# Two banded layers on one core: inverse roots from GpSimd to VectorE, some norm columns from ScalarE to GpSimd, no bias pass in layer two, and a written order for each layer

## The chip, the cores and the metric

The kernel runs on one core of a Trainium2 chip. A core has TensorE (PE, with its weight loads, PEld), VectorE (DVE), ScalarE (ACT), GpSimd (POOL) and SyncE (SP, which here only issues DMAs). Each engine executes its own queue in order. The metric is the device time of one execution in microseconds. Before the change three runs took 4815.11, 4811.23 and 4803.99 us; the median is 4811.23 us. One more execution was taken with the profiler and is the source of every other time below.

## The reference

The input x is 512 x 512 positions with 64 channels. Two layers follow each other, and each is `x = x + conv(_gn(x))`: `_gn` normalizes the channels in 32 groups of two over all positions, and `conv` computes, per position:

```python
xn = _ln(x, norm_scale, norm_bias)                              # over 64 channels
left  = (xn @ Wl + bl) * mask * sigmoid(xn @ Wlg + blg)         # 64 -> 128
right = (xn @ Wr + br) * mask * sigmoid(xn @ Wrg + brg)
out_gate = sigmoid(xn @ Wog + bog)
out = _banded_ingoing(left, right, WIN)       # row i: sum over rows i-4..i+4 of right
out = _ln(out, out_norm_scale, out_norm_bias) * out_gate        # over 128 hidden channels
return out @ Wo + bo                                            # 128 -> 64
```

So each position needs two inverse square roots per layer: one for the norm over 64 input channels and one for the norm over 128 hidden channels.

## The kernel before

**Tiles.** A *unit* is a tile `z` of 128 partitions by 8 columns by 64 channels: 64 rows of the image at 8 columns of its left half on partitions 0 to 63, and the same rows at 8 columns of its right half on partitions 64 to 127. Nine blocks of 64 rows, two chunks of 128 columns in each and 16 units in a chunk make 288 units per layer. An *out* is the same 8 columns on their way out, also 288 per layer. A buffer `RO` holds the projected right side of almost two chunks, and after the band step the same place holds its result.

**Steps.** `layer` (L739) runs a loop over steps t. Step t takes unit t through the projections (`right`, `right_gate`, `right_end`), transposes unit t+1 (`transposed`, `kept`), normalizes unit t+2 (`inner_norm`, L436) and, further ahead, applies the group norm to a unit (`affine`, L427: one multiplication by `ga`, one addition of `gb`) and collects its statistics (`inner_stats`). The band product of a chunk (`mix`, L567, 16 matmul groups and two copies of 128x512 back to `RO` for each) is spread over the steps of the next chunk: per 16 steps six have two of these bands, four have one and six have none. An out with number t leaves LAG = 30 steps after its chunk began: `out_stats` (four statistics instructions), `norm` (L631, one step ahead: eight ScalarE instructions of 128x128, one per column), `gates` and `gated` (matmul and sigmoid of the output gate), `turned` (transposes), `times_gate`, `end` (last product) and, a step later, `ended` (adds the product to the residual tile `XR` and issues the store). In layer one `sums` also accumulates the statistics of the next layer's group norm on PE.

**Inverse roots.** Every fourth step `solve` (L598) takes the variances that have been collected, usually 32 columns of inputs and 32 of outs, so tiles of 128x64. Five small VectorE instructions prepare variances, negated means and a first guess by integer arithmetic; then `rsqrt` (L134) runs ten instructions on GpSimd, and two more there multiply by the mask. All lie in SBUF. `inner_norm` and `norm` read the result `rs` (and `nm`) of the group.

**Residual.** `fetch` loads the 8 columns of the layer's input again into one of four tiles `XR`. `biased` (L698) adds a constant row to it on GpSimd, in both layers: `bo`, and a shift that keeps the intermediate image near zero mean.

**PSUM.** Eight banks. In layer one: three single banks that take turns, two pairs of banks that take turns, and one bank that holds the sums. In layer two: four single banks and two pairs. `right` and `transposed` use pairs; `gates`, `turned`, `end` and both halves of each `mix` use single banks.

**Order.** The instructions are issued through `en`, which keeps program order on every engine, so the text of the loop body (L835 to L910) is the order of every queue. Both layers use the same text. SP's queue issues per step the loads of `z`, `XR`, `A` and `zg` ahead of the body, and the stores of `later` (in `kept`) and of the image (in `ended`).

Of the kernel before, what the change touches and what calls it, by code (L numbers as in the profile page):

```python
# [8 lines left out]
F32 = mybir.dt.float32  # L9
# [7 lines left out]
P = 128  # L17
WIN = 4
# [12 lines left out]
LN_EPS = 1e-6  # L31

# [47 lines left out]
def tile_two_banded_layers(  # L80
# [35 lines left out]
    nc.vector.memset(all_ones, 1.0)  # L116
    ones_row = const.tile([1, P], F32, name="ones_row")
# [16 lines left out]
    def rsqrt(o: bass.AP, v: bass.AP, vec=nc.vector, e=nc.vector):  # L134


        p, n = v.shape
        t, u = (
            sm.tile([P, 3 * NB], F32, tag=f"rsqrt{i}", name="rsqrt", bufs=1)[:p, :n]
            for i in range(2)  # L140
        )
        vec.tensor_scalar(
            o.bitcast(I32), v.bitcast(I32), -0.5, float(0x5F3759DF), ALU.mult, ALU.add
        )
        e.tensor_tensor(t, o, o, ALU.mult)
        e.tensor_tensor(t, t, v, ALU.mult)
        e.tensor_scalar(u, t, -10.0 / 3.0, None, ALU.add)
        e.tensor_tensor(t, t, u, ALU.mult)
        e.tensor_scalar(t, t, 5.0, None, ALU.add)
        e.tensor_tensor(o, o, t, ALU.mult)  # L150
        e.tensor_tensor(t, o, o, ALU.mult)
        e.tensor_tensor(t, t, v, ALU.mult)
        e.tensor_scalar(t, t, -27.0 / 1024.0, 0.5625, ALU.mult, ALU.add)
        e.tensor_tensor(o, o, t, ALU.mult)


    PARTS = (
        ("right", 2 * H), ("left", 2 * H), ("gate", H), ("Wo", D), ("ob", 1), ("add", 2 * D),
# [60 lines left out]
    def solve_layer(i: int, f: dict, r: dict, tmp, half: bass.AP):  # L219
# [36 lines left out]
        add = r["add"].rearrange("p (t c) -> p t c", c=D)  # L256
        nc.vector.tensor_copy(add[:, 0, :], pb[:, :D])
# [15 lines left out]
        nc.vector.tensor_tensor(r["m2"], r["m"], r["m"], ALU.mult)  # L273

# [7 lines left out]
    def shifted(i: int, r: dict, tmp):  # L282
        add = r["add"].rearrange("p (t c) -> p t c", c=D)
        if i == 0:

            bias = tmp.tile([P, G], F32, name="bias")
            nc.vector.tensor_reduce(
                bias, add[:, 0, :].rearrange("p (g t) -> p g t", t=2), AX.X, ALU.add
            )
            nc.vector.scalar_tensor_tensor(bias, bias, 0.5, total, ALU.mult, ALU.add)  # L290
            spread(shift, bias)
        op = ALU.add if i else ALU.subtract
        nc.vector.tensor_tensor(add[:, 0, :], add[:, 0, :], shift, op)
        nc.vector.tensor_copy(add[:, 1, :], add[:, 0, :])


# [6 lines left out]
    shift = const.tile([P, D], F32, name="shift")  # L303
# [4 lines left out]
    def group_affine(mean: bass.AP, var: bass.AP, pool):  # L308

        ve = pool.tile([P, D], F32, name="g_ve")  # L310
        nc.vector.tensor_scalar(ve, var, GN_EPS, None, ALU.add)
        rsqrt(ga, ve)
        nc.vector.scalar_tensor_tensor(gb, mean, -1.0, ga, ALU.mult, ALU.mult)
# [113 lines left out]
    def affine(u: Unit, engine):  # L427

        engine.tensor_tensor(u.z, u.z, mid(ga, JU), ALU.mult)
# [6 lines left out]
    def inner_norm(u: Unit):  # L436
        z = u.z.rearrange("p (k t) c -> p k t c", t=2)
        m = u.mean.unsqueeze(3).broadcast_to([P, JU // 2, 2, D])
        en.gpsimd.tensor_tensor(z, z, m, ALU.subtract)
# [127 lines left out]
    def mix(c: int, A: bass.AP, h0: int) -> list:  # L567
# [6 lines left out]
        ph = [one_bank().rearrange("i (h t j) -> i h t j", h=q, t=2) for s in range(2)]  # L574
# [23 lines left out]
    def solve(w: dict, ins: list, outs: list, sti, sto):  # L598

        ni, no = len(ins) * JU, len(outs) * JU  # L600
        v = sm.tile([P, 3 * NB], F32, tag="var", name="var", bufs=1)[:, : ni + no]
        r = sm.tile([P, 3 * NB], F32, tag="rs", name="rs", bufs=3)[:, : ni + no]
        if ni:
            en.vector.tensor_scalar(
                v[:, :ni].rearrange("p (k t) -> p k t", t=2), sti[:, : ni // 2, 2::3],
                1.0 / D, LN_EPS, ALU.mult, ALU.add,
            )
            for n, u in enumerate(ins):
                u.rs = r[:, n * JU : (n + 1) * JU]
        if no:  # L610

            js = slice(outs[0].m, outs[0].m + no)
            vo = v[:, ni:]
            en.vector.scalar_tensor_tensor(
                vo.rearrange("p (k t) -> p k t", t=2), sto[:, :, 2::3], 1.0 / H,
                w["m2"][:, js].rearrange("p (k t) -> p k t", t=2), ALU.mult, ALU.mult,
            )
            en.vector.tensor_scalar(vo, vo, LN_EPS, None, ALU.add)
            nm = sm.tile([P, NB], F32, tag="nm", name="nm")[:, :no]
            en.vector.tensor_scalar(  # L620
                nm.rearrange("p (k t) -> p k t", t=2), sto[:, :, 1::3], -1.0, None, ALU.mult
            )
        rsqrt(r, v, en.vector, en.gpsimd)
        if no:
            ro = r[:, ni:]
            en.gpsimd.tensor_tensor(ro, ro, w["m"][:, js], ALU.mult)
            en.gpsimd.tensor_tensor(nm, nm, ro, ALU.mult)
            for n, o in enumerate(outs):
                o.rs, o.nm = ro[:, n * JU : (n + 1) * JU], nm[:, n * JU : (n + 1) * JU]
# [417 lines left out]
```

## Time and profile before

| | |
|---|---|
| median of 3 runs | 4811.23 us |
| profiled execution | 4808.51 us, span 4806.5 us |
| busy, whole span | PE 3796.6, DVE 3929.9, ACT 3708.4, POOL 3817.1 us |
| DMA | 983.63 MB, mean 205 GB/s |
| full-load part of layer one, 600 to 2300 us | PE 1555, DVE 1459, ACT 1521, POOL 1560 us busy of 1700 |
| full-load part of layer two, 2900 to 4600 us | PE 1432, DVE 1511, ACT 1492, POOL 1576 us busy of 1700 |

All operations of the loop carry one line, L373, since a helper issues them; they are told apart by the names of their tiles. `z<-z,ga` reads: writes z, reads z and ga. `on<-RO,nm,rs` is `norm`, `ZH<-bank,pack,gate` is `times_gate`, `XR<-XR,fewer` and `XR<-XR,pack` are `biased`, `RO<-banks,sg` is `right_end`, `RO<-bank` are the copies of `mix`, `zT` is `kept`, `sto` and `sti` are statistics. In a group's line the number after the bar is the busy time in us, then the mean duration of one instruction in ns, then the idle time of the engine just ahead of these instructions and what ended it. In a line of the timeline the first number is the start in us and the second how long the piece lasts; the idle time ahead of it stands in brackets.

### The profile page before, as it was taken

How to read it: one execution, taken by the hardware profiler on the slowest of the kernel's cores; microseconds unless marked ns; L12 is line 12 of the kernel's file. 1: busy time of each engine (PE TensorE's matmuls, PEld its weight loads, DVE VectorE, ACT ScalarE, POOL GpSimd, SP SyncE). 2: the span in 40 equal slices, each digit the busy share in tenths (PEclk: the TensorE clock that was granted, in tenths of full speed). 3: DMA queues.
4: the chain of work that ended last, by engine and by line, in shares of the span. 5: the costliest groups of instructions: out<-in, count | busy, mean ns of one | idle time of the engine just before them, and what ended most of it. 6: DMA issues, size and time to landing. Idle time of an engine off the chain costs nothing. (4 is left out here: it accounts for less than half of the span.)

```text
span 4806.5 us, 193543 instructions
## 1 busy us (share of the span) xinstructions
PE 3796.6 (79%) x76306; PEld 3293.0 (69%) x76306; DVE 3929.9 (82%) x9635; ACT 3708.4 (77%) x8732; POOL 3817.1 (79%) x4739
## 2 busy tenths in 40 slices
PE   1025799989999999999985478888888888888888
PEld 0024688878888887888854467777777777777775
DVE  6954788888888888888867478888888888888887
ACT  0013689888888898989883268888888888888899
POOL 0035999999999999999734589999999999999964
PEclk9997999999999999999997689999999999999999
DMA  7859677777777777777763967777777777777876
GB/s 299 336 178 108 172 212 213 215 210 215 211 209 210 211 214 212 214 212 215 199 170 100 105 168 212 216 214 209 217 213 215 213 213 218 210 216 211 222 200 179
DMA packets 1437651, 983.63 MB, mean 205 GB/s; under 512 B 167202, under 2 KB 1284424, under 8 KB 1432392
## 3 DMA queue, kind: packets, MB, share of 16 engines
q1 hardware_dynamic: 1432064, 969.75, 73.6%
q8 instruction: 604, 9.90, 0.9%
q14 instruction: 303, 2.48, 0.2%
q10 hardware_dynamic: 4680, 1.50, 0.1%
HBM read 658.42 MB, written 312.46 MB: 202 GB/s over the span
## 5 line engine op out<-in xcount | busy, mean ns | idle before, releaser
L373 ACT ACTIVATE on<-RO,nm,rs 128x128 f32<-128x128 f32 x4608 | 1927.7, 496 | 15.3 <-PE bank L373 9.9
L373 PEld LDWEIGHTS banks<-pack,zT 64*128 64x128 f32 x18576 | 1251.3, 195 | 549.5 <-ACT zT L373 288.9
L373 PE MATMUL banks<-pack,zT 64*128 64x128 f32 x18576 | 1365.6, 289 | 272.8 <-ACT zT L373 222.6
L373 DVE TENSOR_TENSOR RO<-banks,sg 128x512 f32<-128x512 f32 (+1 forms) x1188 | 795.3, 673 | 228.3 <-POOL sg L373 116.2
L373 DVE SCALAR_TENSOR_TENSOR ZH<-bank,pack,gate 128x448 f32<-128x448 f32 (+1 forms) x1152 | 741.6, 685 | 173.3 <-PE bank L373 97.3
L373 ACT ACTIVATE sg<-banks 128x512 f32<-128x512 f32 (+1 forms) x1188 | 698.0, 589 | 188.6 <-PE banks L373 188.2
L373 DVE BATCH_NORM_STATS2 sto<-RO 128x6 f32<-128x256 f32 x2304 | 800.8, 411 | 3.7
L373 POOL TENSOR_TENSOR z<-z,gb 128x512 f32<-128x512 f32 x536 | 684.8, 1278 | 42.0
L373 PE MATMUL bank<-RO,A 64*64 64x128 f32 x18432 | 706.0, 292 | 3.9 <-ACT RO L373 2.4
L373 PE MATMUL bank<-pack,ZH 128*64 128x64 f32 x18432 | 694.6, 231 | 5.0 <-ACT gate L373 4.1
L373 POOL TENSOR_TENSOR z<-z,ga 128x512 f32<-128x512 f32 x536 | 685.6, 1279 | 3.2 <-DMA z<-mid_x 1.9
L373 POOL TENSOR_TENSOR z<-z,rs 128x512 f32<-128x512 f32 x586 | 619.3, 1057 | 46.0
L373 DVE COPY RO<-bank 128x512 f32<-128x512 f32 x576 | 398.4, 692 | 310.6 <-PE bank L373 307.3
L373 PEld LDWEIGHTS bank<-pack,ZH 128*64 128x64 f32 x18432 | 612.6, 143 | 47.3 <-ACT gate L373 8.5
L373 POOL TENSOR_TENSOR z<-z,sti 128x512 f32<-128x512 f32 x586 | 627.9, 1072 | 0.0
L373 PEld LDWEIGHTS bank<-RO,A 64*64 64x64 f32 x18432 | 582.0, 142 | 43.0 <-ACT RO L373 4.1
L373 ACT ACTIVATE gate<-bank 128x448 f32<-128x448 f32 (+1 forms) x1152 | 565.8, 545 | 34.5 <-PE bank L373 32.0
L373 ACT ACTIVATE zT<-banks 128x512 f32<-128x512 f32 (+1 forms) x1084 | 463.5, 481 | 139.6 <-PE banks L373 128.9
L373 PE MATMUL bank<-zg,pack 64*128 64x448 f32 (+1 forms) x2304 | 564.3, 556 | 4.6 <-DMA zg<-later 4.6
L373 ACT COPY RO<-bank 128x512 f32<-128x512 f32 x576 | 333.2, 579 | 282.3 <-PE bank L373 282.1
L373 PE MATMUL banks<-ident,z 64*128 64x64 f32 x4336 | 254.1, 233 | 359.2 <-DVE RO L373 336.9
L373 DVE BATCH_NORM_STATS2 sti<-z 128x6 f32<-128x128 f32 x2344 | 500.5, 280 | 15.2 <-POOL z L373 14.2
(144 smaller groups left out, 3908.6 us busy)
## 6 DMA issues: line engine op xcount, KB each, us to landing
later<-zT SPq DMA_DIRECT2D x576, 256.0 KB
A<-left_of SPq DMA_DIRECT2D x1152, 128.0 KB
zg<-later SPq DMA_DIRECT2D x576, 256.0 KB
z<-in_x_dram SPq DMA_DIRECT2D x576, 128.0 KB
z<-mid_x SPq DMA_DIRECT2D x576, 128.0 KB
gn_x<-in_x_dram SPq DMA_DIRECT2D x16, 4096.0 KB
XR<-in_x_dram SPq DMA_DIRECT2D x448, 112.0 KB
mid_x<-XR SPq DMA_DIRECT2D x448, 112.0 KB
```

What stands on the lines that cost most here:

```text
L373: return lambda *a, **k: tc.keep_in_program_order(f(*a, **k))
```

## The change

Six things change together.

1. `solve` returns two parts. `prepare` issues on ScalarE one activation that writes the inputs' variances to `var` in SBUF, and two that write the outs' variances and negated means to a PSUM bank. `roots` issues on VectorE 14 instructions in place of five on VectorE and twelve on GpSimd. Its operands alternate between a PSUM bank and SBUF, with at most one SBUF tensor as input of each.
2. `norm` gives the last column (layer one) or the last two columns (layer two) of each out to GpSimd, as one `tensor_scalar` of 128x128 per column.
3. `biased` is no longer called in layer two: `both`, the sum of the two layers' `bo`, is added in layer one, and `mid_stats` takes the second layer's `bo` out of the statistics with six small VectorE instructions. The shift is gone.
4. In layer one both halves of a band lie in one pair of banks; in layer two they stay in two single banks.
5. In layer one the second copy of a second band goes to ScalarE.
6. The loop body is read from a list, one per layer. `affine` and `inner_norm` are split in two calls each, so that the list can place them apart. `prepare` ("solve on a") and `roots` ("solve on d") stand near the end of the step.

```diff
+FIRST = [
+    ("out stats", 2), "gates", "gated", ("project", 0), ("project", 4), "turn",
+    ("sigmoid", 0), ("out stats", 3), "scale", ("right", 0), ("sigmoid", 4),
+    ("norm", (0, 4)), "norm columns", "centre", "move", "last product", ("right", 4),
+    "times gate", "rescale", "transpose", ("out stats", 99), "inner stats", "keep", "solve",
+    "end", ("band", 0), ("copy a", 0), "sums", "bias", ("band", 1), ("copy b", 0),
+    ("solve on", "a"), "scale next", "move next", ("norm", (4, 8)), ("copy a", 1),
+    ("solve on", "d"), ("copy b", 1),
+]
+SECOND = [
+    ("out stats", 3), "scale", ("out stats", 2), "gates", ("project", 0), "gated",
+    ("sigmoid", 0), ("project", 4), ("out stats", 99), ("right", 0), ("sigmoid", 4), "turn",
+    ("norm", (0, 4)), "last product", "norm columns", "centre", "scale next", "rescale",
+    "times gate", "transpose", ("band", 0), "keep", "move next", "end", ("right", 4),
+    ("copy b", 0), "inner stats", "solve", "move", ("copy a", 0), ("band", 1),
+    ("solve on", "a"), ("copy b", 1), ("copy a", 1), ("norm", (4, 8)), ("solve on", "d"),
+]
...
-        ph = [one_bank().rearrange("i (h t j) -> i h t j", h=q, t=2) for s in range(2)]
+        if APART[0 if stats else 1]:
+            pb = [one_bank() for s in range(2)]
+        else:
+            two = two_banks()
+            pb = [two[:, s * 512 : (s + 1) * 512] for s in range(2)]
...
+        def prepare():
+            held.extend((one_bank(), temporary("var")))
+            bank, v = held
+            if ni:
+                en.scalar.activation(
+                    pairs(v[:, :ni]), sti[:, : ni // 2, 2::3], AF.Identity, bias=ln_eps,
+                    scale=UP / D,
+                )
+            if no:
+                en.scalar.copy(pairs(bank[:, 6 * NB : 6 * NB + no]), sto[:, :, 2::3])
+                en.scalar.mul(pairs(bank[:, 7 * NB : 7 * NB + no]), sto[:, :, 1::3], -1.0)
+
+        def roots():
+            bank, v = held
+            y, s = bank[:, :n], bank[:, 3 * NB :][:, :n]
+            t, u = temporary("rsqrt_t"), temporary("rsqrt_u")
+            vec = en.vector
+            if no:
+                vo, mean = (bank[:, k * NB : k * NB + no] for k in (6, 7))
+                vec.tensor_tensor(vo, vo, w["m2"][:, js], mult)
+                vec.tensor_scalar(v[:, ni:], vo, LN_EPS * UP, None, add)
+            vec.tensor_scalar(
+                y.bitcast(I32), v.bitcast(I32), -0.5, float(0x5F3759DF - 2**31), mult, add
+            )
+            vec.tensor_tensor(u, y, v, mult)
+            vec.tensor_tensor(t, y, u, mult)
+            vec.tensor_tensor(s, y, u, mult)
+            vec.scalar_tensor_tensor(u, t, -10.0 / 3.0, s, add, mult)
+            vec.scalar_tensor_tensor(y, u, 5.0, y, add, mult)
+            vec.tensor_tensor(u, y, v, mult)
+            vec.tensor_tensor(t, y, u, mult)
+            c = -0.5625 * 1024.0 / 27.0
+            if ni:
+                vec.scalar_tensor_tensor(r[:, :ni], t[:, :ni], c, y[:, :ni], add, mult)
+            if no:
+                vec.scalar_tensor_tensor(y[:, ni:], t[:, ni:], c, y[:, ni:], add, mult)
+                vec.tensor_tensor(ro, y[:, ni:], w["m"][:, js], mult)
+                vec.tensor_tensor(nm, mean, ro, mult)
...
+            if pool:
+                en.gpsimd.tensor_scalar(to, of, rs, nm, ALU.mult, ALU.add)
+            else:
+                en.scalar.activation(to, of, AF.Identity, bias=nm, scale=rs)
...
+                elif name == "norm" and t + 1 in outs:
+                    lo, hi = n
+                    norm(outs[t + 1], lo, min(hi, JU - nv), False)
+                elif name == "norm columns" and t + 1 in outs:
+                    norm(outs[t + 1], JU - nv, JU, True)
```

Here `nv` is 1 in layer one and 2 in layer two, and `APART` is false in layer one and true in layer two.

## The prediction

> **What bounds the kernel now.** I read the page's busy table first (four engines within 82% and 77%: no verdict), then the stretches of full load, then GpSimd's groups in them, the waits and the timeline.
>
> ```profile
> 600.00:2300.00 1700.00, 1555.34 (x32978) 1372.73 (x32977) 1459.31 (x3598) 1521.02 (x3542) 1560.42 (x1885) 0.98 0.76 212
> 2900.00:4600.00 1700.00, 1432.20 (x29446) 1255.82 (x29439) 1510.81 (x3630) 1492.26 (x3568) 1576.47 (x1907) 0.96 0.77 214
> ```
>
> After the window come its length, then PE, PEld, DVE, ACT, POOL, the granted clock, the DMA share and GB/s. GpSimd is highest in both layers (92 and 93%). Its groups between 800 and 2300 us:
>
> ```profile
> L373 POOL TENSOR_TENSOR z<-z,ga 128x512 f32<-128x512 f32 x208 | 265.9, 1278 | 0.0
> L373 POOL TENSOR_TENSOR z<-z,gb 128x512 f32<-128x512 f32 x207 | 264.6, 1278 | 16.2
> L373 POOL TENSOR_TENSOR XR<-XR,fewer 120x512 f32<-120x512 f32 x188 | 223.5, 1189 | 0.3 <-DMA XR<-in_x_dram 0.2
> L373 POOL TENSOR_TENSOR z<-z,sti 128x512 f32<-128x512 f32 x208 | 219.7, 1056 | 0.0
> L373 POOL TENSOR_TENSOR z<-z,rs 128x512 f32<-128x512 f32 x208 | 216.9, 1043 | 16.3
> L373 POOL TENSOR_SCALAR rsqrt<-rsqrt 128x64 f32<-128x64 f32 x156 | 50.9, 326 | 13.6
> L373 POOL TENSOR_TENSOR rsqrt<-rs 128x64 f32<-128x64 f32 x104 | 30.4, 292 | 47.1 <-DVE rs L373 43.0
> ```
>
> Its only real wait is 43.0 us, for VectorE's first guess; the other idle time is gaps of about 0.08 us. The five large operations and their gaps are 1247 us, 5.99 per step over 208 steps. The root groups (seven, of which two stand above) are 190 us busy and 90 idle: 280 / 52 solves = 5.4 us, 1.35 per step. Together they fill the window. GpSimd is the bound, and the others wait for what it delays:
>
> ```profile
> 1508.51 0.18 DVE L373 SCALAR_TENSOR_TENSOR var<-sto,pack 128x32 f32<-128x32 f32 x1
> 1508.72 1.20 DVE L373 TENSOR_SCALAR var<-var 128x32 f32<-128x32 f32 x1
> 1510.23 0.29 POOL L373 TENSOR_TENSOR rsqrt<-rs 128x64 f32<-128x64 f32 x1 [0.35 <-DVE rs L373]
> 1510.87 0.35 PEld L373 LDWEIGHTS banks<-ident,z 64*128 64x128 f32 x8 [2.83 <-POOL rsqrt L373]
> 1514.54 0.25 POOL L373 TENSOR_TENSOR nm<-nm,rs 128x32 f32<-128x32 f32 x1
> ```
>
> A solve also makes VectorE wait: a 128x32 operation that takes 0.18 us elsewhere took 1.20 beside a GpSimd operation, and PE stood still 2.8 us. Period of 16 steps, from the last product of the same step: layer one 116.2 us (1442.59 to 1558.83), layer two 114.3 (half of 3507.19 to 3735.74):
>
> ```profile
> 1442.59 1.15 PE L373 MATMUL bank<-pack,ZH 128*64 128x64 f32 x32
> 1558.83 1.15 PE L373 MATMUL bank<-pack,ZH 128*64 128x64 f32 x32
> 3735.74 1.15 PE L373 MATMUL bank<-pack,ZH 128*64 128x64 f32 x32
> ```
>
> What the other engines need of a period is its length times the share in which they don't wait in the table of waits. Layer one (1500 us): PE waits 127, so 106.4; ACT 161: 103.7; DVE 208: 100.1. Layer two: PE 236: 96.3; ACT 186: 100.1; DVE 160: 102.1.
>
> **The change, per 16 steps (four solves).**
>
> *Roots.* GpSimd loses 4 x 5.4. VectorE loses five instructions (77.6 us / 52 = 1.49 per solve in layer one; 114.6 / 53 = 2.16 in layer two, where contention weighs more) and gains 14 dependent ones. The nearest row is the root chain that runs on VectorE between the layers, same width, twelve instructions in 2.87 us from the first's start to the next operation's:
>
> ```profile
> 2563.90 0.20 DVE L142 TENSOR_SCALAR ga<-on 128x64 int32<-128x64 int32 x1
> 2564.12 0.22 DVE L145 TENSOR_TENSOR rsqrt<-ga 128x64 f32<-128x64 f32 x1
> 2566.77 0.68 DVE L373 TENSOR_TENSOR z<-z,ga 128x512 f32<-128x512 f32 x1
> 2560.60 0.21 DVE L931 TENSOR_TENSOR on<-acc,ident 64x64 f32<-64x64 f32 x1
> ```
>
> 0.239 each, 3.35 per solve; the last line has a PSUM operand and takes no longer. Bounds: 0.11 each (spacing of independent ones, 2 us less) to 0.50 (mean of the `var` rows beside GpSimd, 7.0 per solve). I take 3.35. Net +7.4 (layer one), +4.8 (layer two). The chain stands at the step's end; behind it queue the next step's statistics and first `right_end`, which frees the banks that PE needs.
>
> [...]
>
> *Prepare.* Three small activations. Nearest row 128x128 at 0.42 busy; I take 0.3 (0.2 to 0.42): ACT +3.6. It waits for the last statistics, with two norm columns and band copies behind it.
>
> *Norm columns.* ACT loses 0.42 per column (697.0 / 1661): -6.7, -13.4. GpSimd pays between 0.33 (128x64 scalar row) and 1.04 (a 128x512 row, 18 times on `sg`); by width and a gap I take 0.5: +8, +16. New wait: the columns need the previous out's transposes done, so GpSimd can no longer run ahead of PE's step; centring and rescaling queue behind, but their reader is the transpose one step later, some 4 us of cover. Without the cover, that wait returns to PE.
>
> [...] Here the giver is ACT, so 0.5 against 0.42 buys balance. [...]
>
> *Bias.* GpSimd loses 1.19 x 16 in layer two: its four operations on `z` remain, 268.9 + 268.4 + 220.5 + 218.0 us and 33 of gaps in 2900 to 4400 us, 4.80 per step over 210. In that layer's tail its wait for the `XR` loads (40 us after 4620) goes too; next in line is `ended`, which reads the same tile a step later, so I count nothing there. The six operations in `mid_stats` stand in the open between the layers: 6 x 0.239 = 1.4 us, less the few that set up the shift.
>
> *Band copies.* Layer one: six of 16 copies move, DVE -3.7 (spacing 0.61), ACT +3.5. Pairs instead of single banks: the pair users per step become projections 2, transpose 1, band 1; hidden behind the six PE groups of a step while copies keep pace; a late copy holds the next projection, and at the worst one copy (0.6 us) per two-band step shows, 6 x 0.6 = 3.6 per period.
>
> *Orders, bank rings.* No work, only waits; bounded below nothing by the better packing and above by the slower case among the rivals. On SP the stores stay behind the same instructions (`later` behind `keep`, the image behind `end`) and the loads ahead of the body; the number of issues per step does not change. The DMA share of 0.76 and 0.77 rises with the pace to about 0.81; a wait of PE, ACT, DVE or POOL for a load is at most 0.2 us now in full load, so I take nothing; the bound above is a late `z` load holding GpSimd, which the tails show for `XR` (up to 12.5 us once).
>
> Needs after, layer one: PE 106.4, POOL (5.99 + 0.5) x 16 = 103.8, DVE 100.1 + 7.4 - 3.7 = 103.8, ACT 103.7 - 6.7 + 3.5 + 3.6 = 104.1. Layer two: DVE 106.9, PE 96.3, POOL (4.80 + 1.0) x 16 = 92.8, ACT 90.3. The bound engine now gets 97% of the time (43 us lost of 1500); with that, 106.4 / 0.97 = 109.7 and 106.9 / 0.97 = 110.2. Gain 6.5 and 4.1 per period. Units and outs run together in steps 30 to 287, 16.1 periods per layer: 105 + 66 = 171 us. Ends: the last 16 steps of layer two go at 4.02 us, ACT-bound on eight columns (16 x 0.6 = 10); the steps before and layer one's tail 10; the two starts (GpSimd 90% busy) 5 each. Sum 171 + 30 - 1 = 200. The profiled execution's 4808.5 less 200 is 4608; the median lies 3 us above it: **4610 us**.
>
> **Rivals.**
>
> - *Better packing* (0.15): PE's 106.4 holds stretched weight loads. From the timeline, undisturbed steps take 7.95 (two bands) and 6.27 (one); with 5.45 for none, 6 x 7.95 + 4 x 6.27 + 6 x 5.45 = 105.5. At 106 in both layers: 16.1 x 18.5 + 30 = 328, so 4480.
> - *Waits take the place* (0.16): four near-equal engines get 94%: 113.2, 113.7; 16.1 x 3.6 + 30 = 88: 4725. A norm column at 0.75 in layer one gives (5.99 + 0.83) x 16 / 0.97 = 112.5, much the same.
> - *Slower: the root chain is not covered* (0.14). Place: the end of each fourth step, 0.9 of prepare plus 3.35, with PE waiting for the banks behind it, as it waited 2.8 us at 1510. Layer one's 105.5 + 4 x 4.25 = 122.5 against 116.2; layer two's undisturbed 102 (7.16, 6.25, 5.69 per step) + 17 = 119. 16.1 x 11 - 30 = +147: 4960. It decides from 2.7 us (layer one) and 3.1 (layer two) exposed per solve. Against it: roots are needed only by the next step's norms and rescaling, after its sigmoids, 3.5 us in.
> - *No difference* (0.02).
>
> Forecast's own case, 4540 to 4680: 0.53. A measurement tells 0.2%, some 10 us. Faster 0.15 + 0.16 + 0.53 = 0.84. Below 4480 I leave 0.07; the slower case starts at 4822 and reaches to 4960, and I keep the range to 4820, leaving 0.13.
>
> **What would show it.** GpSimd's `rsqrt` groups gone, VectorE with about 14 instructions of 0.2 per solve and no `var` row near 1 us; GpSimd's busy share in layer two near 84%, VectorE's near 95% and highest; PE's waits for POOL (75 and 61 us per 1500) gone; 16 steps near 110 us in both layers; 128x128 columns on POOL near 0.45. Wrong if PE's waits for VectorE grow beyond the present 97 and 167 us per 1500, if columns cost 1 us, or if the chain's instructions take 0.4 or more.

## The result and the profile after

The changed kernel takes 4767.63 us (median of 4 runs, 4746.72 to 4776.52), the kernel before 4813.17 us beside it (4803.99 to 4817.25): a ratio of 0.9897, 95% interval 0.9879 to 0.9915. It is 1% faster, where 4% was forecast. The profiled execution takes 4769.15 us, span 4767.2.

The two stretches of full load after, with the same columns as before (window, length, PE, PEld, DVE, ACT, POOL, clock, DMA share, GB/s):

```profile
600.00:2300.00 1700.00, 1581.22 (x32602) 1373.64 (x32602) 1466.38 (x3985) 1507.07 (x3528) 1421.86 (x1398) 0.98 0.76 210
2900.00:4600.00 1700.00, 1495.45 (x29730) 1302.58 (x29726) 1542.81 (x4175) 1424.44 (x3296) 1281.06 (x1429) 0.96 0.78 215
```

GpSimd is no longer the fullest engine: 1422 and 1281 us in place of 1560 and 1576. PE is now, in layer one (1581 us), and VectorE in layer two (1543), but the time hardly fell. Some of the groups between 800 and 2300 us:

```profile
L381 POOL TENSOR_SCALAR on<-RO,rs,nm 128x128 f32<-128x128 f32 x207 | 93.4, 451 | 232.0 <-PE bank L381 113.9 <-ACT sg L381 110.4 <-DVE nm L381 6.3
L381 DVE TENSOR_TENSOR rsqrt_u<-bank,var 128x64 f32<-128x64 f32 x102 | 22.9, 224 | 3.5
L381 DVE SCALAR_TENSOR_TENSOR bank<-rsqrt_t,bank 128x32 f32<-128x32 f32 x51 | 10.0, 196 | 1.8
L381 PE MATMUL bank<-zg,pack 64*128 64x448 f32 (+1 forms) x824 | 253.0, 605 | 62.8 <-DMA zg<-later 55.0 <-DVE sto L381 3.2 <-DVE sti L381 2.8
```

The norm column costs 0.451 us, the root chain's instructions 0.19 to 0.23 us, and GpSimd waits 232 us, which is its slack. The last line is new: the matmuls of `gates` (`bank<-zg,pack`) wait for the load of `zg`, the gate's input that `recall` reads back from memory. The table of waits (engine, what it waited to do, for whom; total, times, longest) between 2900 and 4400 us has more of it. In the kernel before there was none, neither there nor between 800 and 2300 us:

```profile
PE bank L381 <- DMA zg<-later: 96.8, 48, 4.4
PEld bank L381 <- DMA zg<-later: 50.0, 22, 4.5
```

One such wait in the timeline (start, duration):

```profile
1544.31 0.55 SPq L381 DMA_DIRECT2D zg<-later  x1
1548.12 1.87 PE L381 MATMUL bank<-zg,pack 64*128 64x448 f32 x4 [3.02 <-DMA zg<-later]
1549.75 2.62 PE L381 MATMUL banks<-pack,zT 64*128 64x128 f32 x32
1550.04 0.98 ACT L381 ACTIVATE gate<-bank 128x448 f32<-128x448 f32 x2 [3.31 <-issue]
1552.20 0.69 DVE L381 TENSOR_TENSOR RO<-banks,sg 128x512 f32<-128x512 f32 x1 [4.00 <-ACT sg L381]
1553.06 0.45 POOL L381 TENSOR_SCALAR on<-RO,rs,nm 128x128 f32<-128x128 f32 x1 [4.91 <-ACT sg L381]
```

SP issued the load at 1544.31, and PE took its data 3.8 us later, after 3.0 us of standing still. ACT, VectorE and GpSimd then wait in turn. In the new lists `gates` is among PE's first work of a step; before it stood behind the first `right` products.

Pair the n-th `zg` load of a trace with the n-th out's gate product, and take the time from the start of the issue to the start of the product. In the two stretches of full load its median was 9.7 and 8.6 us before and is 6.3 and 5.3 us now. Where PE waited for the load now, this time was at least 2.99 us, so no load that PE waited for was there sooner. Before, one product in 475 started less than 4 us behind the issue; now 90 of 472 do. This one was the shortest before, with 3.85 us and no wait:

```profile
3613.06 0.56 SPq L373 DMA_DIRECT2D zg<-later  x1
3616.91 0.92 PE L373 MATMUL bank<-zg,pack 64*128 64x448 f32 x4
```

The stall has a second price, in the granted clock (column behind the busy times):

```profile
1548.10:1551.50 3.40, 3.38 (x24) 2.64 (x26) 0.10 (x1) 0.98 (x2) 0.05 (x1) 0.56 0.91 255
```

For 3.4 us behind the stall the clock is 0.56, and the projections take 2.62 us, where they took 1.95 to 2.18 us in the three steps before. A shorter pause has the same behind it: 1.92 us ahead of 3209.41, with a clock of 0.50 from 3209.99 to 3213.40, and projections of 3.39 us.

Where did the 39 us of the profiled executions go? Measured from the first to the 257th last product of a layer, 16 steps went from 115.4 to 116.3 us in layer one and from 114.0 to 113.9 in layer two: 11 us more over 16 such periods in each layer. The ends gained 50 us: the first last product comes 27 us earlier (519.9 in place of 547.0), the stretch from layer one's last to layer two's first of them is 18 us shorter (261.5 in place of 280.0), the two tails 2.6 and 1.9. So the steady state, in which 171 us were forecast, gained nothing.

### The profile page after: what moved, and what is told of

It reads as the page before. It is cut to its first block, busy times and chain, and to the rows that moved or that the text cites. A ratio compares the mean times of both kernels' runs of the same rounds, so it can differ in the third digit from the quotient of the medians.

```text
span 4767.2 us, 193179 instructions
## 1 busy us (share of the span) xinstructions
PE 3885.2 (81%) x76306; PEld 3337.2 (70%) x76306; DVE 4007.1 (84%) x10943; ACT 3608.6 (76%) x8410; POOL 3274.7 (69%) x3427
## 3 DMA queue, kind: packets, MB, share of 16 engines
q1 hardware_dynamic: 1432064, 969.69, 74.4%
## 5 line engine op out<-in xcount | busy, mean ns | idle before, releaser
L381 ACT ACTIVATE on<-RO,nm,rs 128x128 f32<-128x128 f32 x3744 | 1588.5, 492 | 91.8 <-DVE nm L381 44.9
L381 PEld LDWEIGHTS banks<-pack,zT 64*128 64x128 f32 x18576 | 1304.4, 203 | 380.6 <-ACT zT L381 204.4
L381 POOL TENSOR_SCALAR on<-RO,rs,nm 128x128 f32<-128x128 f32 x864 | 383.9, 451 | 975.7 <-ACT sg L381 504.5
L381 PE MATMUL bank<-zg,pack 64*128 64x448 f32 (+1 forms) x2304 | 727.3, 615 | 213.5 <-DMA zg<-later 193.8
L381 PE MATMUL bank<-pack,ZH 128*64 128x64 f32 x18432 | 667.3, 226 | 17.8 <-DVE nm L381 16.7
L381 PEld LDWEIGHTS bank<-pack,ZH 128*64 128x64 f32 x18432 | 587.4, 138 | 60.9 <-DVE nm L381 24.2
L381 PE MATMUL bank<-ident,on 64*128 64x64 f32 x9216 | 453.8, 227 | 27.5 <-ACT gate L381 25.0
L381 PEld LDWEIGHTS bank<-zg,pack 64*128 64x128 f32 x2304 | 240.5, 191 | 336.5 <-DMA zg<-later 62.7
L381 PEld LDWEIGHTS bank<-ident,on 64*128 64x128 f32 x9216 | 426.5, 141 | 69.6 <-ACT gate L381 44.7
L381 DVE TENSOR_TENSOR XR<-bank,XR 120x512 f32<-120x512 f32 (+1 forms) x576 | 390.9, 679 | 2.5 <-PE bank L381 1.2
```

What stands on the lines that cost most here:

```text
L381: return lambda *a, **k: tc.keep_in_program_order(f(*a, **k))
```

## The experiments

Theory A: the late `zg` loads, which the new order's early `gates` expose, ate the gain. Theory B: SP's queue of issues (97 us of issue time per 16 steps: 1255 and 1276 us of 1500) took GpSimd's place as the bound, and any load left in it will be waited for. Theory C: the root chain, or the pairs of banks, hold PE. "16 steps" is always measured as above, given as layer one / layer two; before 115.4 / 114.0, after 116.3 / 113.9. Ratios are against the kernel before on the same chip.

### The `zg` load on ACT's queue

```diff
 def recall(o: Out):
-        en.sync.dma_start(o.t, later[o.at])
+        en.scalar.dma_start(o.t, later[o.at])
...
                 elif name == "gated" and o:
                     gated(o)
+                    if t + 2 in outs:
+                        recall(outs[t + 2])
```

> The load of `zg` goes to ACT's queue, right behind the gated product that frees its buffer, and SP loses one issue of five to nine per step (about 0.55 us each, 9 us of every 16 steps). Theory A: about as in the run with the earlier load, 4620 to 4680 us, ACT giving back some 0.5 us per step where it is not covered. Theory B: SP's issue time falls from about 103 to 94 us per 16 steps, so this run gains more than the earlier load on the same queue, 4600 to 4680 against 4740 to 4780. Theory C: 4720 to 4770 in both.

Measured: 4634.55 us, ratio 0.9641 (0.9626 to 0.9655), 16 steps 112.9 / 109.5.

```profile
600.00:2300.00 1700.00, 1626.23 (x33725) 1407.00 (x33723) 1507.59 (x4113) 1536.85 (x3645) 1460.23 (x1436) 1.00 0.83 217
2900.00:4600.00 1700.00, 1553.57 (x30426) 1335.34 (x30427) 1589.12 (x4294) 1443.71 (x3407) 1252.47 (x1421) 0.98 0.84 220
```

PE's waits for `zg` are gone (2.3 us of weight loads in 1500 are left in layer one, none in layer two), the median time from issue to product is 12.2 and 11.5 us, the clock is 1.00 and PE is 96% busy in layer one. 133 us come back: this is the better version, and it beats both kernels. The issue costs ACT 0.33 us a step. A and B are not yet apart.

### The same load a step earlier on SP's queue

```diff
-            if t + 2 in outs:
-                recall(outs[t + 2])
+            if t + 3 in outs:
+                recall(outs[t + 3])
...
-    ztg = ctx.enter_context(tc.tile_pool(name="ztg", bufs=2))
+    ztg = ctx.enter_context(tc.tile_pool(name="ztg", bufs=3))
-    zp = ctx.enter_context(tc.tile_pool(name="zp", bufs=12))
+    zp = ctx.enter_context(tc.tile_pool(name="zp", bufs=11))
```

> The changed kernel with the `zg` loads left on SP's queue but issued one step earlier (three buffers in place of two; the pool of `z` tiles goes from 12 to 11 to make room). With the load on ACT's queue the time fell to 4635 us. Theory A (only the lateness of `zg` mattered): about the same here, 4630 to 4670, PE's waits for `zg` under 10 us per 1500. Theory B (SP's queue is full; an issue less on it is what helped): 4720 to 4780, with waits for the other loads of the queue (`XR`, `A`, `z`) in place of those for `zg`. If a pool of 11 is too small, waits of POOL or PE for `z` loads show it.

Beside 12 `z` tiles a third `zg` buffer finds no room in SBUF: 2.06 kB per partition were left for a pool that takes 3.75.

Measured: 4684.63 us beside 4840.09 of the kernel before on this chip, ratio 0.9680 (0.9664 to 0.9696); 16 steps 112.1 / 109.4, as fast as with the load on ACT's queue, with SP's issues as many as in the changed kernel. B falls as the bound: what counted was when the load started. Some waits for `zg` remain (10.5 us per 1500 in layer one, 37.7 in layer two), and GpSimd waits 112 us for `z` in layer two, which cost it nothing visible. The total is 0.4% behind, at the layers' starts, where a pool of 11 and the chip are not told apart.

### `gates` behind the first `right` products

```diff
-    ("out stats", 2), "gates", "gated", ("project", 0), ("project", 4), "turn",
-    ("sigmoid", 0), ("out stats", 3), "scale", ("right", 0), ("sigmoid", 4),
+    ("out stats", 2), ("project", 0), "gates", ("sigmoid", 0), "gated", ("project", 4), "turn",
+    ("out stats", 3), "scale", ("right", 0), ("sigmoid", 4),
...
-    ("out stats", 3), "scale", ("out stats", 2), "gates", ("project", 0), "gated",
-    ("sigmoid", 0), ("project", 4), ("out stats", 99), ("right", 0), ("sigmoid", 4), "turn",
+    ("out stats", 3), "scale", ("out stats", 2), ("project", 0), "gates", ("sigmoid", 0),
+    "gated", ("project", 4), ("out stats", 99), ("right", 0), ("sigmoid", 4), "turn",
```

> The changed kernel with the gate products moved behind the first four `right` products (and the first sigmoid ahead of the gated product); loads are where they were. Theory A: the load gets about 2 us more; of the waits for `zg` of 1.2 to 4.4 us at least half go (under 30 and 45 us per 1500), 4680 to 4740 us. Theory B: no change, 4740 to 4780, waits for other loads instead. Theory C: no change in time, waits for VectorE instead; gated products now come later, which could also cost up to 1 us per step in ACT's order (4780 to 4840).

Measured: 4736.13 us, ratio 0.9873 (0.9843 to 0.9903); 16 steps 113.6 / 113.7.

```profile
PE bank L381 <- DMA zg<-later: 34.1, 27, 2.4
PEld banks L381 <- ACT zT L381: 115.1, 130, 1.6
PE banks L381 <- ACT zT L381: 90.3, 91, 1.4
```

These are its waits between 2900 and 4400 us. In layer one the waits for `zg` fell from 55 to 7.7 us and the period by 2.6, as A says. In layer two they fell too, but the period stayed: `zT`, ACT's copies of the transposes, came later instead. The order has other reasons for early gates; bringing the load forward does not touch them.

### One load for both halves of `z`

```diff
-            for e, j in enumerate((u.j, LH + u.j)):
-                en.sync.dma_start(u.z[e * S : (e + 1) * S], src[rows, j : j + JU, :])
+            en.sync.dma_start(
+                u.z, strided(src, (u.blk.s * L + u.j) * D, (LH * D, 2), (L * D, S), (1, JU * D))
+            )
```

> The changed kernel with the two loads of a `z` tile made one (same bytes), `zg` left on SP where it was: SP loses as many issues per step as when `zg` went to ACT (one, 0.55 us). Theory A: the `zg` load follows one issue sooner, 0.55 us; waits of 1.2 to 4.4 us shrink by that much, 4735 to 4770 us. Theory B: the same relief as the load on ACT's queue, so 4620 to 4690 us.

Measured: 6581.28 us, ratio 1.3608 (1.3588 to 1.3628), far outside both theories, so it tells nothing about them. The page's line of SP's queue, of the changed kernel and then of this one (packets, MB, share of 16 engines):

```profile
q1 hardware_dynamic: 1432064, 969.69, 74.4%
```

```profile
q1 hardware_dynamic: 1414784, 969.62, 54.1%
```

The bytes are the same, but there are 17,280 packets fewer, all of them packets of 4 bytes (72,702 in place of 89,982; of every other size there are as many as before). With 576 loads in place of 1152, that is what it takes if each old load ended with 16 small packets and each new one with 2 (1152 x 16 - 576 x 2 = 17,280), an estimate from these counts. The queue's share of 16 engines fell from 74.4 to 54.1% of a span 1.38 times as long; how a load of either form is spread over them was not shown.

### The kernel before with `zg` on ACT's queue

```diff
-        en.sync.dma_start(o.t, later[o.at])
+        en.scalar.dma_start(o.t, later[o.at])
...
                 gated(outs[t])
+                if t + 2 in outs:
+                    recall(outs[t + 2])
```

> The kernel before with its `zg` load on ACT's queue behind the gated product. It shows no wait for `zg`, GpSimd is full, and its ACT waits in the open for some 160 us per 1500. Theory A: nothing to win, 4795 to 4830 us. Theory B (SP's queue bounds both kernels): faster, 4700 to 4780 us.

Measured: 4863.77 us beside 4840.09, ratio 1.0057 (1.0042 to 1.0072); 16 steps 116.8 / 115.1. The kernel before does not gain, it pays for the issue on ACT. The late load is the new kernel's own problem. This speaks against B once more.

The next runs take the parts back one at a time, from the version with `zg` on ACT's queue (4635 us, 112.9 / 109.5).

### Roots back on GpSimd

```diff
         def roots():
-            bank, v = held
+            v, t, u = held
+            e = en.gpsimd
+            e.tensor_tensor(t, r, r, mult)
+            e.tensor_tensor(t, t, v, mult)
+            e.tensor_scalar(u, t, -10.0 / 3.0, None, add)
...
```

`prepare` likewise holds the five VectorE instructions of before, and all temporaries lie in SBUF.

> The version with `zg` on ACT's queue (4635 us; 16 steps take 113.0 us in layer one and 109.3 in layer two), with the inverse roots put back on GpSimd in the form of the kernel before (five small operations on VectorE, twelve on GpSimd, temporaries in SBUF), at the same two places of the written order. By the sum of the prediction GpSimd then needs 5.99 + 0.45 + 1.35 per step in layer one, 124.7 per 16 steps, and 4.80 + 0.90 + 1.35 in layer two, 112.8; at 97% that is 128.5 and 116.3, so over 18 periods a layer some 400 us more: about 5000 us (4900 to 5080). If GpSimd's full window in the kernel before was no bound (its small root operations run in gaps that remain): under 4720 us.

Measured: 5159.85 us, ratio 1.0737 (1.0718 to 1.0757). 16 steps 130.0 / 121.7. The forecast range is passed, and not by the mechanism of the sum: between 600 and 2300 us GpSimd is busy 1462.64 of 1700 us, not full. The line that shows the cost, between 800 and 2300 us:

```profile
ACT on L381 <- POOL nm L381: 257.7, 46, 7.0
```

In this order ACT's norm columns wait for the end of the chain, up to 7 us. So the move of the roots is worth some 525 us here, because the chain's result comes sooner, and not as work taken off a full engine. How much of that is the chain's length (3 us on VectorE in place of 5.4) and how much its place in GpSimd's queue, no run separates.

### Root temporaries in SBUF

```diff
-            held.extend((one_bank(), temporary("var")))
+            wide = sm.tile([P, 8 * NB], F32, tag="wide", name="wide", bufs=1)
+            held.extend((wide, temporary("var")))
```

and 11 `z` tiles to make room.

> The version with `zg` on ACT's queue (4635 us; 113.0 and 109.3 us per 16 steps), the root chain's 256 columns of PSUM temporaries in an SBUF tile instead (the pool of `z` tiles is 11, not 12, to make room, which in the run with earlier `zg` loads went with 35 us lost at each layer's start). If PSUM operands make the small operations no longer, as the row between the layers suggests, and the bank's user is hidden: instructions stay at 0.19 to 0.23 us, 16 steps at 112 to 113.5 and 108.5 to 110, time 4635 to 4710. If the bank taken from the ring of three is what holds layer one's PE: 16 steps there 109 to 111. [...]

Measured: 5116.35 us, ratio 1.0641 (1.0624 to 1.0659), 16 steps 129.4 / 120.3: none of the expected cases. VectorE's groups between 800 and 2300 us:

```profile
L381 DVE TENSOR_TENSOR rsqrt_u<-wide,var 128x64 f32<-128x64 f32 x92 | 57.0, 619 | 3.2
L381 DVE TENSOR_TENSOR wide<-wide,pack 128x32 f32<-128x32 f32 x46 | 51.7, 1125 | 0.0
L381 DVE TENSOR_SCALAR var<-wide 128x32 f32<-128x32 f32 x46 | 46.9, 1019 | 1.6
L381 DVE TENSOR_SCALAR wide<-var 128x64 int32<-128x64 int32 x46 | 36.6, 795 | 1.6
```

The same instructions take 0.19 to 0.23 us with a PSUM operand. All twelve groups of the chain sum to 285.9 us over 46 solves, 6.2 each, against 156.3 over 53, 2.95 each, with the bank. These four groups hold the chain's first instructions, which run while GpSimd works on `z` in SBUF. Of the chain's 644 instructions in this stretch 148 take over 0.4 us, and every one of these ends within 0.15 us of the end of a GpSimd operation, as here:

```profile
1531.76 1.28 POOL L381 TENSOR_TENSOR z<-z,gb 128x512 f32<-128x512 f32 x1
1531.77 1.31 DVE L381 TENSOR_SCALAR var<-wide 128x32 f32<-128x32 f32 x1
```

They are the `var` rows of the kernel before again. Of the other 496 most run while GpSimd waits for the roots, and take 0.18 to 0.23 us with all operands in SBUF. With a PSUM operand the same instructions show no such wait: in the version with the bank 676 of the chain's 742 instructions between 800 and 2300 us run while GpSimd works, and none takes over 0.23 us. Why the slow ones end with GpSimd's operation was not shown. Of the 482 us some 440 lie in the steady state, 16 periods of 16.6 and 10.9 us more: the chain is 3.3 us longer four times per period, and the rest is what waits for it; PE stood up to 5.8 us for `right_end` behind it. Another 47 us lie at the layers' starts, as they did with 11 `z` tiles in the run with earlier `zg` loads.

### Bands of layer one in single banks

```diff
-APART = (False, True)
+APART = (True, True)
```

> The version with `zg` on ACT's queue (4635 us) with each band's product of layer one in two single banks as before, not in a pair. If pairs cost what the prediction's bound allows (3.6 us per 16 steps): 109.5 to 111 in layer one, 4570 to 4610 us. If pairs are hidden or even help (four single banks per two-band step from a ring of three, besides the other six users): 4630 to 4720 us. If PE alone bounds layer one (96% busy): 4625 to 4645.

Measured: 4835.49 us, ratio 1.0058 (1.0043 to 1.0074), 16 steps 125.4 / 110.1. The pairs are worth 200 us in layer one: they help, and by more than the second case allowed. Waits between 800 and 2300 us:

```profile
PEld bank L381 <- DVE ZH L381: 98.2, 279, 0.8
PEld bank L381 <- ACT RO L381: 63.1, 93, 1.8
```

PE's weight loads wait for readers of the three single banks, which `gates`, `turned`, `end`, the roots and now four band halves share.

### Norm columns back on ACT

```diff
-NV = (1, 2)
+NV = (0, 0)
```

> The version with `zg` on ACT's queue, norm columns all on ACT. By the sum: ACT 104.1 + 6.7 = 110.8 per 16 steps in layer one, at 97% 114.2 (now 113.0), in layer two 103.7, below the present 109.3: 4635 to 4665 us. If the columns are what frees the path (ACT's last columns hold the transposes): 4700 to 4750. If GpSimd's new wait for the previous transposes costs more than ACT's relief brings: under 4630.

Measured: 4728.28 us, ratio 0.9843 (0.9820 to 0.9865), 16 steps 114.6 / 112.8. The columns are worth 94 us, the second case. Layer one's 114.6 is the sum's 114.2. In layer two the sum left ACT slack at 103.7, and the period grew by 3.3 all the same. The last 31 steps of layer two grew from 137.5 to 147.6 us. So the columns are worth the 10 us that the prediction gave to that tail; but the tail took 138.3 us in the kernel before, and gained 0.8 us by all parts together.

### The bias pass back in layer two

```diff
-    "times gate", "transpose", ("band", 0), "keep", "move next", "end", ("right", 4),
+    "times gate", "transpose", ("band", 0), "keep", "move next", "end", "bias", ("right", 4),
```

> The version with `zg` on ACT's queue with the bias pass put back on GpSimd in layer two, behind `ended` (its addend is then counted twice, so the output is off by that constant; the work is that of before). By the sum GpSimd needs (4.80 + 0.90 + 1.19) x 16 = 110.2 per 16 steps, at 97% 113.7 against 109.3 now, over 18 periods 79 us: about 4715 us (4690 to 4740). If GpSimd's slack (1242 of 1650 us busy) swallows 19 us per period: 4635 to 4650.

Measured: 4637.06 us, ratio 0.9644 (0.9628 to 0.9660), 16 steps 112.7 / 110.0.

The same stretch in the version with `zg` on ACT's queue, and then here:

```profile
2900.00:4550.00 1650.00, 1511.00 (x29810) 1306.23 (x29811) 1542.75 (x4168) 1402.01 (x3305) 1241.91 (x1397) 0.98 0.85 221
2900.00:4550.00 1650.00, 1505.11 (x29694) 1300.54 (x29690) 1536.15 (x4147) 1399.75 (x3291) 1518.83 (x1638) 0.98 0.84 220
```

GpSimd goes from 1242 to 1519 us of 1650, 92%, and the time stays. Once the roots are off it, GpSimd swallows the pass: taking it away was worth nothing, and an engine 92% full was no bound.

### Second band's copies on ACT in layer two too

```diff
-SECOND_ON_ACT = (True, False)
+SECOND_ON_ACT = (True, True)
```

> The version with `zg` on ACT's queue, with the second band's copies on ACT in layer two as well: VectorE (1543 of 1650 us busy there) loses six copies of 16 per 16 steps, 3.7 us, ACT (1402 of 1650) gains 3.5. If VectorE is layer two's bound now: 16 steps from 109.3 to 106 to 108, 4575 to 4615 us. If PE and its waits are: 4625 to 4650 us.

Measured: 4648.26 us, ratio 0.9680 (0.9650 to 0.9710), 16 steps 112.8 / 110.1.

```profile
2900.00:4550.00 1650.00, 1507.85 (x29687) 1306.81 (x29689) 1480.04 (x4057) 1431.62 (x3382) 1242.66 (x1397) 0.98 0.84 220
```

VectorE, the fullest engine of layer two, was relieved (1543 to 1480 us of 1650) and nothing came of it. What holds layer two at 109.5 us stays open: neither VectorE's nor GpSimd's work does. The largest waits of PE there are for GpSimd's norm columns `on` (36.9 us of matmuls and 108.5 of weight loads in 1500), and yet the columns are worth their place.

The last five runs ask what the written orders are worth. They use the changed kernel (with `zg` on SP) and, as one list for both layers, the order of before, with its pieces named as in the lists; layer two's list has no bias and no sums.

### All parts in the order of before, and four variants

```diff
+OLD = [
+    ("out stats", 3), "centre", "rescale", ("project", 0), ("sigmoid", 0), "gates", ("project", 4),
+    "scale", "move", ("out stats", 99), "inner stats", "solve", ("solve on", "a"),
+    ("solve on", "d"), "gated", ("right", 0), "bias", "turn", ("sigmoid", 4), "transpose",
+    "times gate", "scale next", "move next", "last product", ("right", 4), ("band", 0),
+    ("norm", (0, 4)), "norm columns", "keep", "sums", ("copy a", 0), "end", ("norm", (4, 8)),
+    ("band", 1), ("copy b", 0), ("copy a", 1), ("copy b", 1),
+]
```

> All parts of the change (roots on VectorE, PSUM temporaries, norm columns on GpSimd, no bias pass in layer two, pairs of banks) with the order that the kernel before has in both layers. The gate products then stand behind the first `right` products again. Theory A (the new order's early gate products cause the loss): PE's waits for `zg` under 20 us per 1500, and the time below the changed kernel's, 4640 to 4720 us. If the written orders are worth something that the `zg` waits only partly eat: 4770 to 4850. Theory C (the parts themselves, above all the root chain, are what costs): 4770 us or more, with PE's waits for VectorE as large as in the kernel before (97 and 167 us per 1500) or larger.

Measured: 5176.96 us, ratio 1.0777 (1.0761 to 1.0793), 16 steps 129.7 / 122.5. Hardly any wait for `zg` (6.6 us in the whole run), and yet 8% slower than before: the third case, and the parts need the new order. Between 800 and 2300 us:

```profile
PEld banks L389 <- DVE RO L389: 198.5, 215, 2.6
DVE RO L389 <- ACT RO L389: 170.7, 118, 1.9
PE banks L389 <- DVE RO L389: 166.3, 176, 2.4
```

*Columns back on ACT in that order*:

```diff
-NV = (1, 2)
+NV = (0, 0)
```

> All parts of the change in the order of before (5177 us), but with the norm columns all on ACT again: what remains in the old order is the roots on VectorE, the three small activations of prepare, the pairs of banks in layer one and the missing bias pass in layer two. If the norm columns on GpSimd were what cost (GpSimd's wait for the previous out's transposes holds centring and rescaling, 320 to 372 us of `on` waits per 1500): 4750 to 4850 us. If it is the root chain standing ahead of the first `right_end` in that order, or the pairs of banks: 5050 to 5200 us; the chain's share is bounded by 52 solves of some 4.3 us per 1500 us, about 130 us per layer, so the root chain alone would give about 5000.

Measured: 5306.27 us beside 4840.09, ratio 1.0969 (1.0953 to 1.0986), 16 steps 130.6 / 125.9: slower than either case expected. The columns help there as well. In its timeline the chain, 14 instructions, runs from 1505.9 to 1509.2, then the first `right_end`, and PE stands for it:

```profile
1509.12 0.68 DVE L389 TENSOR_TENSOR RO<-banks,sg 128x512 f32<-128x512 f32 x1
1509.94 0.69 PE L389 MATMUL banks<-ident,z 64*128 64x64 f32 x8 [2.39 <-DVE RO L389]
1510.57 1.97 PE L389 MATMUL bank<-pack,ZH 128*64 128x64 f32 x32
```

This is the wait of the prediction's slower rival, at another place of the step, with the half clock behind it (0.50 from 1509.94 to 1513.40; the last product takes 1.97 us, not 1.15). It made theory D: move the chain.

*Chain at the end of the step*:

```diff
-    "scale", "move", ("out stats", 99), "inner stats", "solve", ("solve on", "a"),
-    ("solve on", "d"), "gated", ("right", 0), "bias", "turn", ("sigmoid", 4), "transpose",
+    "scale", "move", ("out stats", 99), "inner stats", "solve", "gated", ("right", 0), "bias",
+    "turn", ("sigmoid", 4), "transpose",
...
-    ("band", 1), ("copy b", 0), ("copy a", 1), ("copy b", 1),
+    ("band", 1), ("copy b", 0), ("copy a", 1), ("solve on", "a"), ("copy b", 1),
+    ("solve on", "d"),
```

> The run in the order of before (5177 us, 16 steps 129 and 123 us), with one thing moved: prepare and the root chain go from ahead of the gated product and the first `right_end` to the end of the step. Theory D (there the chain holds the first `right_end`, its banks and with them PE some 2.4 us, after which PE runs on at about half its clock for some microseconds; that is the prediction's slower rival): 16 steps fall to 114 to 118 and 112 to 116, time 4740 to 4880 us. Rival (it is the rest of the old order, the copies and products behind each other with pairs of banks, that costs): 5050 to 5200 us.

Measured: 5262.95 us, ratio 1.0950 (1.0933 to 1.0966), 132.9 / 126.0, slower than either case expected. D falls in this form. The statistics of the next step and the chain still stand ahead of the same `right_end`, and the wait is longer:

```profile
1513.72 0.69 PE L389 MATMUL banks<-ident,z 64*128 64x64 f32 x8 [4.69 <-DVE RO L389]
```

*First `right_end` ahead of statistics and chain* (the chain where it was in the first of these runs):

```diff
-    "scale", "move", ("out stats", 99), "inner stats", "solve", ("solve on", "a"),
-    ("solve on", "d"), "gated", ("right", 0), "bias", "turn", ("sigmoid", 4), "transpose",
+    "scale", "move", ("right", 0), ("out stats", 99), "inner stats", "solve", ("solve on", "a"),
+    ("solve on", "d"), "gated", "bias", "turn", ("sigmoid", 4), "transpose",
```

> The run in the order of before (5177 us, 16 steps 129 and 123 us) with the first `right_end` moved ahead of the statistics and the root chain on VectorE. Theory D in its new form (all that VectorE does ahead of the first `right_end`, 3 us of statistics and 3.3 of roots, holds the pair of banks that the transposes need, and the transposes stand early in that order): PE's waits of 365 and 376 us per 1500 for VectorE fall to about half, 16 steps to 115 to 120, time 4760 to 4900 us. Rival (the second `right_end`, the copies, or ACT's and GpSimd's places hold PE in that order): 5080 to 5200 us.

Measured: 5159.81 us, ratio 1.0729 (1.0713 to 1.0745), 133.2 / 117.9. Layer two falls into the expected 115 to 120, layer one gets worse; there PE's weight loads wait for `nm` (83 us) and for the gates (91 us) instead. D explains part of layer two only.

*Single banks for layer one's bands*:

```diff
-APART = (False, True)
+APART = (True, True)
```

> The run in the order of before (5177 us, 16 steps 129 us in layer one, 123 in layer two) with each band's product of layer one in two single banks, as the kernel before has it. If pairs, which make the two copies of a band follow each other, are what costs in that order: layer one falls to 117 to 122, layer two stays, 4980 to 5060 us. If they help there as they do in the new order: layer one 130 to 140, 5190 to 5380. If the time stays within 20 us of 5177, they are not what separates the two orders.

Measured: 5090.14 us, ratio 1.0588 (1.0572 to 1.0603), 123.9 / 122.5, a smaller gain than the first case expected. In that order the pairs cost 5.7 us per 16 steps of layer one, where in the new order they save 12.5. With a pair, VectorE's copy of the second half waits for ACT's of the first: the 170.7 us above. With single banks that wait is gone, and in the new order with pairs it is 0.7 us. What else makes this order slow with the new parts was not settled.

## Why the prediction was right and wrong

The direction was right, and so were the prices of the root chain and the norm columns; the size was wrong: 4610 us forecast, range 4480 to 4820, 4767.63 measured.

- **Bound before.** GpSimd's root chain was the right thing to remove: put back into the version with `zg` on ACT's queue it costs 525 us. That GpSimd's full queue bounded the kernel before is read from its trace alone, where it hardly waits; in the run with the roots put back GpSimd is 86% busy in layer one and ACT waits 258 us of 1500 for `nm`, and the bias pass filled GpSimd to 92% at no cost.
- **Prices.** Chain 2.95 us busy and some 3.3 with its gaps, forecast 3.35; column 0.451, forecast 0.5; PE's matmuls wait less for VectorE, from 97 to 28 us (layer one) and from 172 to 65 us (layer two) per 1500, as forecast. But its weight loads, which hardly waited for VectorE before, now do so for 129 and 45 us. The 75 and 61 us of waits for `rsqrt`, which are gone, were also waits of weight loads; at the one that the prediction shows, the matmuls' own row (below) names VectorE's `right_end`. So these rows alone don't tell how much of PE's waiting the move of the roots took away. The slower rival (chain not covered) did not come in the new order; a place like it was seen in the old one.

```profile
1510.90 0.46 PE L373 MATMUL banks<-ident,z 64*128 64x64 f32 x8 [2.72 <-DVE RO L373]
```

- **The step that failed: *Orders, bank rings*,** "a wait of PE, ACT, DVE or POOL for a load is at most 0.2 us now in full load, so I take nothing". It looked for a late `z` load holding GpSimd. The late load was `zg`, holding PE. The prediction counted the issues on SP, which did not change, and not the distance from each issue to its reader, which the new lists shortened by moving `gates` to the head of PE's step: from a median of 9.7 and 8.6 us to 6.3 and 5.3. The distance could be read off the trace before: 8.6 us in layer two's median and 3.85 at the shortest, with SP issuing for 96 us of 115. This term is 133 us by the medians (4767.63 less 4634.55) and 2.56% of the time before by the ratios (0.9897 less 0.9641), 123 us.
- **What is left of the gap.** Without that wait 16 steps are 112.9 and 109.5; forecast 109.7 and 110.2. Layer two's size is right by luck: the sum has VectorE as the bound there, and VectorE relieved of copies (1543 to 1480 us of 1650) brought nothing; the bias pass, priced at 1.19 x 16 = 19 us of GpSimd, was worth nothing either. Layer one is 3.2 us over: PE, 96% busy there, does 108 us of work in a period of 112.9, not 106.4. The sum also started from one period of 116.2 us, where the mean of 16 is 115.4: 13 us. The ends gave 60 us (27 at the start, 21 between the layers, 10 in layer one's tail, 1 in layer two's), forecast 30; why the starts gained so much, no run shows. So 16 x (2.55 + 4.57) = 114 in the steady state and 60 at the ends make the 174 us between the profiled spans (4806.5 less 4632.9).
- **Pairs of banks**, "hidden ... at the worst" 3.6 us per period: wrong in sign. They save 12.5 us per period of layer one, as the ring of three single banks would otherwise hold PE. The prediction counted the pairs' users and not the single banks'.
- **PSUM temporaries.** The prediction went by the row between the layers, which was right: the chain's instructions take 0.19 to 0.23 us with a PSUM operand, and 0.18 to 0.23 with all operands in SBUF where GpSimd waits for the roots. What was missed is that the prediction's own upper bound, 0.50 each and 7.0 per solve beside GpSimd, is the case without the bank (6.2), and that keeping out of it is worth most of 482 us here.
- **Rivals.** Waits take the place (4725) and no difference (the 4811 of before) lie equally near to the 4767.63, some 43 us off. The steady state in fact made no difference. Waits did take the place, but by a late load and not by four near-equal engines.

## What to carry to other kernels

When an order changes, list for each load the time from its issue to its reader, before and after, not only the number of issues; a reader moved to the head of a step needs its load a step earlier. The small chain of VectorE operations beside a busy GpSimd took 2.95 us with its temporaries in a PSUM bank and at most one SBUF input each, and 6.2 with all of them in SBUF, so here they belong in the bank. An engine that is 92% full need not be a bound (the bias pass cost nothing), and the same part can save in one order what it costs in another (pairs of banks: 12.5 us saved, 5.7 lost), so parts and order are priced together.

## What was not expected of the hardware

- Writing two loads as one, with a dimension of size two in front, took the kernel from 4768 to 6581 us at the same bytes (969.69 and 969.62 MB), with the share of 16 DMA engines down from 74.4 to 54.1% of the span.
- A PE stall of 3.02 us was followed by 3.4 us at a clock of 0.56, so that it cost more than itself: the projections behind it took 2.62 us and not 1.95 to 2.18. A stall of 1.92 us was followed by 3.4 us at 0.50 too. In the full-load stretches of the changed kernel there are 47 slow stretches; in the 3.4 us ahead of one PE was busy for 0.39 of the time and its longest pause was 2.1 us (both medians).
- The issue of one `zg` load takes 0.39 to 0.54 us of SP's queue (medians between 1400 and 1600 us in the kernels after and before), and 0.326 of ACT's.
- VectorE operations of 0.2 us lasted 0.6 to 1.1 us when their operands lay in SBUF beside GpSimd's, also one with a single tensor input (`var<-wide`, 1.019).
